# Two outlook-attention layers: first copies and zeros ahead of the loop, two weights' tables, a first normalisation on two engines, held projections

## The chip, the cores and the metric

The kernel runs on one core of one Trainium2 chip. The core has five engines that run their own instruction streams: TensorE (PE, with its weight loads shown apart as PEld), VectorE (DVE), ScalarE (ACT), GpSimd (POOL) and SyncE (SP), which here does nothing but issue DMAs. They wait for one another through semaphores. The metric is the device time of one execution in microseconds; lower is better. Here it was 3481.11 us, the median of 3 runs (3480.89 to 3484.68).

## The reference: what is computed

The input x is 8 images of 56 x 56 tokens with 384 channels, in float32. Two layers follow one another, each with a residual, and each works on a group normalisation of its input (32 groups of 12 channels, mean and variance over a whole image):

```python
x = x + L0(gn(x))
x = x + L1(gn(x))

# L0: 12 heads of 32 channels, 3x3 neighbourhoods on both sides (9 x 9 weights per head)
v = x @ Wv.T ; v_unf = the 3x3 neighbourhood of v (zero padded)        # (b, n, 9, 12, 32)
attn = softmax((x @ Wa.T).reshape(b, n, 12, 9, 9) * 32 ** -0.5)         # over the last axis
out = einsum('bnhpq,bnqhd->bnphd', attn, v_unf)                         # 9 results per token
y = fold(out)       # each of the 9 is added at its neighbour's place
return y @ Wo.T

# L1: 6 heads of 64 channels, one result per token
a = softmax((x @ W_attn + b_attn).reshape(b, n, 6, 9))
y = einsum('bpKhd,bphK->bphd', 3x3 neighbourhoods of (x @ W_v + b_v), a)
return y @ W_proj + b_proj
```

In both layers a result pixel is therefore a weighted sum of v over a small neighbourhood (5 x 5 in layer 0, after the fold; 3 x 3 in layer 1), with weights of its own for each pixel and head.

## The kernel before

**Units of work.** Images are taken in pairs (4 pairs). A pair has R = 112 rows (two images of 56) and W = 56 columns. A step of layer 0's loop (line 901) is one column of one pair, so the loop has 4 x 56 = 224 steps and 3 more for what lags behind (`LAG`). A column has 112 tokens and a matmul takes 128, so 7 columns carry the eighth along and every eighth step has no attention matmuls of its own (`NTILE`). What a column's weights and values are used for is a *patch*: PX = 7 columns of a pair, 8 patches to a pair, 32 in all. Layer 1 walks over the same 32 patches as groups of 7 steps.

**Tables in DRAM.** A weighted sum over a neighbourhood is computed as matmuls whose stationary side is a weights' matrix that is mostly zero. It is made by writing weights into a table in DRAM with one arrangement and reading it back with another. `vtab0` and `vtab1` hold values with zero margins, `ztab0[n]` and `ztab1[n]` weights; patch number n of a layer uses weights' table n modulo `NTAB` (3), lines 738, 781, 1113 and 1130. Before a table is used, its margins and gaps must be zero: `clear_v` (line 218, 3 DMAs) and `clear_weights` (line 229, 6 DMAs) send them from a tile of zeros on SP's queue. `clears` (line 239) lists at which step of layer 0's loop which table is cleared, and `upkeep` (line 855) issues what is due, one step at a time. Other tensors in DRAM: `xTs`, x transposed (channels on partitions); `x1s`, the result of layer 0; `lgtab`, layer 1's logits; `lasts`, parts of the eighth columns.

**The start.** Pair 0 is loaded in 14 blocks of 4 columns (672 KB each), transposed on TensorE and kept in SBUF, each block in a place that something else uses later: the tiles `wts`, z, vp, yT, xres, x1t (`homes`, line 489). `keep_block` (line 467) sends a block to `xTs` in DRAM; in the loop `upkeep` sends two in each of steps 0 to 6. At steps 1 and 8 GpSimd zeroes `wts` and the two z tiles, which the blocks must have left. After the last block, `norm_params` (line 269) turns the statistics into a scale and a bias for each channel and image (its square root is ScalarE's, line 298), and `normed` (line 568) applies them: blocks 0 and 1 ahead of the loop (lines 898 and 899), on ScalarE, in pieces of a chunk of 128 channels and one image.

**A step of layer 0.** `attend` (line 591) does three thirds of the attention logits of a column (`bank<-wa_t,xn`, three matmuls over the chunks of channels for each third, six in the profile's count) and its values (`bank<-wv_t,xn`). In the gaps between them `between(n)` (line 921) puts other work: the transposes of the next pair's x (`pt<-ident,xr`; the block xr is loaded by `stats_load` on SP's queue, every third step, one block ahead), the softmax's normalisation and the sums of neighbouring columns on GpSimd (`normalise`, `presum`), the sum over rows by matmul (`pw<-pre,shift`, in `fold`, three steps behind), the write of the weights (`ztab<-wts`) and jobs.

**Jobs.** `Jobs` (line 357) is a queue of closures with a due step; only its head is looked at, and a call `jobs.run(step, n)` runs at most n of those that are due. A step of layer 0 has two or three such places. `fetch` (line 771) reads a patch's weights (`z<-ztab`) and adds its jobs: 4 contractions (`pc<-z,vp`), 6 projections (`po<-yT,wo_t`, each followed on VectorE by the residual's sum `x1t<-po,xres`) and, for a pair's last patch, the next layer's parameters. `later` holds DMAs that are issued at the end of a step.

**The boundary and layer 1.** The last patch of layer 0 is fetched inside layer 1's loop: `last` (line 954) is called at step 0 of it with a due step 5 later (line 1209), so that its jobs and layer 1's first ones share one queue. A step of layer 1 (line 1200) has two places for jobs and one column of projections (`bank<-wc_t,xn`, values and logits together). The logits of a group go to DRAM when the group is done (`keep_logits`, at m = 0 of the next), are read back by rows (`read_logits`), weighed and shared out on VectorE and ScalarE, summed over rows on TensorE (`pw` in `move`, at m = 5), written to `ztab1`, and read as z two groups later.

**What sets the order.** Nearly every instruction is issued through `InOrder` or a helper with `keep_in_program_order`, so each engine and each queue does its work in the order of the program's text; a scheduler places only the few that are not. SP's queue carries nearly all DMAs, in order, and a waiting one holds up what is behind it. GpSimd's queue carries the values' spreads (`vtab<-v`), ScalarE's the logits and layer 1's weights. Line 134 in the profile is that helper, and line 215 is `fill`.

Of the kernel before, what the change touches and what calls it, by code (L numbers as in the profile page):

```python
# [8 lines left out]
F32 = mybir.dt.float32  # L9
AF = mybir.ActivationFunctionType  # L10
# [5 lines left out]
def two_outlook_layers(  # L16
# [35 lines left out]
    P = 128  # L52
# [41 lines left out]
    EP1, FIRST1 = 11, 4  # L94
    SLOT0, SLOT1 = EP0 * ROW0, EP1 * ROW1
    LINE0, LINE1 = SX0 * SLOT0 + ROW0, SX1 * SLOT1 + ROW1
    NTAB = 3

    xf = x.rearrange("b y x c -> (b y) x c")
    of = out.rearrange("b y x c -> (b y) x c")  # L100
# [108 lines left out]
    def fill(table, first, dims, width):  # L209

        src = zeros[: dims[0][1], :width]
        if len(dims) > 1:
            src = src.unsqueeze(1).to_broadcast([dims[0][1], dims[1][1], width])
        tc.keep_in_program_order(
            nc.sync.dma_start(bass.AP(table.tensor, table.offset + first, [*dims, [1, width]]), src)
        )

    def clear_v(table, sx, pad):

        line = sx * C  # L220
        part = line // 12
        fill(table, 0, [[(R + GAP) * line, NPX + 1], [part, 12 * GAP]], part)
        fill(table, GAP * line, [[line, R], [C, pad]], C)
        fill(
            table, ((NPX - 1) * (R + GAP) + GAP) * line + (sx - pad) * C,
            [[line, R], [C, pad]], C,
        )

    def clear_weights(table, line, part, sx, slot, row, first, e, ep):
# [6 lines left out]
        fill(table, top + first * row, [[slot, sx]], row)  # L236
        fill(table, top + (R - 1) * line + (first + e - 1) * row, [[slot, sx]], row)

    def clears():

        yield 3, lambda: clear_v(vtab0, SX0, 2)

        yield 4, lambda: fill(
            ztab0[0], MARGIN * LINE0 + FIRST0 * ROW0, [[LINE0, R], [SLOT0, 2]], E0 * ROW0
        )
        for n, t in enumerate(ztab0):
            yield (5, 2 * PX, 3 * PX)[n], lambda t=t: clear_weights(
                t, LINE0, 366, SX0, SLOT0, ROW0, FIRST0, E0, EP0
            )
        yield 4 * PX, lambda: clear_v(vtab1, SX1, 1)  # L250
        for n, t in enumerate(ztab1):
            yield (5 + n) * PX, lambda t=t: clear_weights(
                t, LINE1, 350, SX1, SLOT1, ROW1, FIRST1, K, EP1
            )

# [8 lines left out]
    def weight(pool, src, n, name, queue=nc.sync):  # L264
        t = pool.tile([P, NCH, n], F32, name=name)
        queue.dma_start(t, src.rearrange("(i p) n -> p i n", p=P))
        return t
# [153 lines left out]
    def layer0(late, pools):  # L421
# [93 lines left out]
        for blk in range(NBLK):  # L515
            if blk + NXR - 1 < NBLK:
                first_load(blk + NXR - 1)
            for i in range(NCH):
                for _ in stats_chunk(0, blk, i):
                    pass  # L520
            if blk == 1:
                wv_t = weight(fixed, wv0, C, "wv0_t", sync)
        for _ in norm_params(stats.pop(0), "0_0", params, 0):
            pass

# [39 lines left out]
                xTs[pair][:, :, blk * XB * R : (blk + 1) * XB * R],  # L565
            )

        def normed(g, chunks, whole=True, shared=True):

            scale, bias = params[g // NBLK]  # L570
            xin, to = xins[g], xns[g // 2 % 2]
            for i in chunks:
                for b in range(IMG):
                    rows = slice(b * H, (b + 1) * H)

                    def put(dst, src):
                        scalar.activation(
                            dst, src, AF.Identity,
                            bias=bias[:, i, b : b + 1], scale=scale[:, i, b : b + 1],
                        )  # L580

                    n = XB - g % 2
                    if whole:
                        put(to[:, i, g % 2 * XB : g % 2 * XB + n, rows], xin[:, i, :n, rows])
                    if shared and g % 2:
                        put(
                            to[:, i, :, R + b * PART : R + (b + 1) * PART],
                            xin[:, i, n, rows].rearrange("p (j y) -> p j y", j=NTILE),
                        )
# [178 lines left out]
                lambda: sync.dma_start(xres[pair, px], xTs[pair][:, :, px * T : (px + 1) * T])  # L768
            )

        def fetch(pair, px, due):

            nm = f"0_{pair}_{px}"
            n_tile = 2
# [64 lines left out]

            for half in range(2):  # L840
                for j in range(NCH):
                    jobs.add(due, lambda half=half, j=j: project_out(half, j))
            if px == NPX - 1:
                def params_part(n):
                    if n == 0:
# [9 lines left out]
        def upkeep(step):  # L855

            pair, c = divmod(step, W)
            if pair == 0:

                for n in (2 * step, 2 * step + 1):  # L860
                    if n < NBLK:
                        keep_block(0, (0, 1, 4, 2, 3)[n] if n < 5 else n)
                if c == 1:
                    gpsimd.memset(wts, 0.0)
                if c == 3:
                    sync.dma_start(wo_t, wo0.rearrange("(i p) n -> p i n", p=P))
                if c == 8:
                    for z in zs:
                        nc.gpsimd.memset(z, 0.0)
            while clearing and clearing[0][0] <= step:  # L870
                clearing.pop(0)[1]()
            if pair + 1 < NPAIR:
                blk, i = divmod(c - 3, NCH)
                if 0 <= c and i == 0 and blk < NBLK - 1:
                    stats_load(pair + 1, blk + 1, sync, xr_tile(pair + 1, blk + 1))
                if NBLK * NCH + 3 <= c < NBLK * NCH + 6:
                    if c == NBLK * NCH + 3:
                        making["0"] = norm_params(stats.pop(pair + 1), f"0_{pair + 1}", params, pair + 1)
                    next(making["0"])
            g, j = divmod(step + 2 * XB, XB)  # L880
            if j < NCH and g < NPAIR * NBLK:
                normed(g, (j,))
            if step < NCH:
                normed(1, (step,), shared=False)
            if j == NCH - 1 and 2 < g + 1 < NPAIR * NBLK and g > 2:
                load(g + 1)
# [8 lines left out]

        vector.on = scalar.on = True
        xins.update({blk: homes[blk] for blk in range(4)})
        normed(0, range(NCH))
        normed(1, range(NCH), whole=False)
        LAG = 3  # L900
        for step in range(NPAIR * W + LAG):
            folding = fold(*divmod(step - LAG, W)) if step >= LAG else iter(())
# [3 lines left out]
            def weigh():  # L906
# [11 lines left out]
                if normal:  # L918
                    keep_v(*divmod(step - 1, W))

            def between(n):

                if n == 0:
                    next(turning, None)
                    weigh()
                    jobs.run(step, 1)
                elif n == 1:
                    next(folding, None)
                    next(turning, None)
                elif n == 2:  # L930
                    jobs.run(step, 1)
                else:
                    for part in summing:
                        next(part)
                    next(folding, None)
                    if step % SB == NTILE:
                        jobs.run(step, 1)
# [15 lines left out]

        def last(due):
            fetch_v(NPAIR - 1, NPX - 1)
            fetch(NPAIR - 1, NPX - 1, due)

        return step + 1, last, late_w

# [329 lines left out]
```

## Time and profile before

| What | Value |
|---|---|
| median of 3 runs | 3481.11 us (3480.89 to 3484.68) |
| the profiled execution | 3478.32 us, span 3476.5 us, mean clock 0.963 |
| TensorE busy | 3228.9 us, 93% |
| TensorE waiting for xr (`pt`), whole run | 46.7 us in 8 waits |
| TensorE waiting for GpSimd's pre (`pw`), whole run | 49.0 us in 16 waits |
| first matmul of layer 0's loop | at 65.99 us |
| layer 0's last patch and layer 1's first group | about 2225 to 2360 us |
| DMA | 859.13 MB, mean 247 GB/s |
| DMA share, 60 to 80 us | 0.00 |

How to read it: a line of the timeline has the start in us, the length in us, the engine (SPq is SP's queue issuing), the line of the program, the operation, what it writes and reads, and in brackets the idle time just before it with the work that ended that wait. A line of the waits has total, number and longest. A row of the windows has the stretch, its length, the busy time and count of each engine, the granted clock of TensorE, the DMA engines' busy share and GB/s. The totals of engines are means over stages that differ: TensorE is busy for nine tenths or more of most slices of the span, and for less at the start, around the boundary of the layers and at the end.

### The profile page before, as it was taken

How to read it: one execution, taken by the hardware profiler on the slowest of the kernel's cores; microseconds unless marked ns; L12 is line 12 of the kernel's file. 1: busy time of each engine (PE TensorE's matmuls, PEld its weight loads, DVE VectorE, ACT ScalarE, POOL GpSimd, SP SyncE). 2: the span in 40 equal slices, each digit the busy share in tenths (PEclk: the TensorE clock that was granted, in tenths of full speed). 3: DMA queues.
4: the chain of work that ended last, by engine and by line, in shares of the span. 5: the costliest groups of instructions: out<-in, count | busy, mean ns of one | idle time of the engine just before them, and what ended most of it. 6: DMA issues, size and time to landing. Idle time of an engine off the chain costs nothing. (4 is left out here: it accounts for less than half of the span.)

```text
span 3476.5 us, 74347 instructions
## 1 busy us (share of the span) xinstructions
PE 3228.9 (93%) x28510; PEld 2202.7 (63%) x28510; DVE 1873.0 (54%) x4780; ACT 1369.4 (39%) x3755; POOL 1367.7 (39%) x1982
## 2 busy tenths in 40 slices
PE   7688999999999998999998999888999999999998
PEld 5456666666666666666666666645666665656665
DVE  5556766666777666677666767532333332323331
ACT  4333444344444343444433443323434333433432
POOL 2544545544545454445454555421222222222220
PEclk7899999999999999999999999998999999999998
DMA  6788988887888687879766868768787878787875
GB/s 184 233 284 287 310 284 260 276 281 253 289 285 298 221 273 266 302 257 301 262 198 215 300 227 267 260 236 216 208 236 207 235 208 226 218 218 220 233 210 140
DMA packets 595753, 859.13 MB, mean 247 GB/s; under 512 B 205798, under 2 KB 470950, under 8 KB 591302
## 3 DMA queue, kind: packets, MB, share of 16 engines
q1 hardware_dynamic: 476806, 682.87, 62.6%
q0 software_dynamic: 59136, 148.12, 13.5%
q10 hardware_dynamic: 59456, 23.40, 2.9%
q8 instruction: 224, 3.67, 0.5%
q14 instruction: 131, 1.07, 0.1%
HBM read 520.28 MB, written 330.40 MB: 245 GB/s over the span
## 5 line engine op out<-in xcount | busy, mean ns | idle before, releaser
L119 PE MATMUL bank<-wa_t,xn 128*128 128x288 f32 x3528 | 981.3, 417 | 7.4 <-ACT xn L134 6.1
L119 PE MATMUL po<-yT,wo_t 128*128 128x448 f32 (+1 forms) x2304 | 827.1, 499 | 27.1 <-DVE x1t L134 24.5
L134 POOL TENSOR_TENSOR at<-at,den 128x972 f32<-128x972 f32 x196 | 440.6, 2248 | 932.8 <-DVE den L134 527.8
L119 PEld LDWEIGHTS bank<-wa_t,xn 128*128 128x128 f32 x3528 | 656.8, 194 | 222.8 <-issue 25.3
L119 PEld LDWEIGHTS po<-yT,wo_t 128*128 128x128 f32 x2304 | 428.9, 192 | 316.9 <-issue 187.8
L134 ACT ACTIVATE at<-at 128x972 f32<-128x972 f32 (+1 forms) x228 | 215.4, 945 | 963.1 <-DVE at L134 962.7
L332 POOL DMA_DIRECT2D vtab<-v x392 | 213.3, 548 | 845.5 <-DVE v L134 801.8
L119 PE MATMUL bank<-wc_t,xn 128*128 128x438 f32 x1176 | 481.9, 546 | 0.0
L134 DVE TENSOR_REDUCE mx<-bank 128x36 f32<-128x324 f32 x588 | 285.0, 485 | 346.2 <-PE bank L119 342.5
L119 PE MATMUL pc<-z,vp 121*32 121x49 f32 (+1 forms) x17664 | 386.0, 221 | 65.5 <-ACT yT L134 25.3
L119 PEld LDWEIGHTS pc<-z,vp 121*32 121x32 f32 (+1 forms) x17664 | 346.7, 123 | 137.6 <-issue 88.9
L119 PE MATMUL bank<-wv_t,xn 128*128 128x384 f32 x1176 | 423.4, 497 | 0.0
L134 DVE TENSOR_TENSOR at<-bank,mx 128x324 f32<-128x324 f32 x588 | 291.3, 495 | 170.9 <-ACT pre L134 58.8
L119 PEld LDWEIGHTS bank<-wc_t,xn 128*128 128x128 f32 x1176 | 216.3, 193 | 171.6 <-issue 165.0
L119 PEld LDWEIGHTS bank<-wv_t,xn 128*128 128x128 f32 x1176 | 222.8, 193 | 137.4 <-issue 15.8
L134 POOL DMA_DIRECT2D vtab<-v x476 | 289.8, 612 | 22.1 <-DMA vtab<-zeros 11.4
L134 ACT COPY yT<-pc 128x294 f32<-128x294 f32 (+2 forms) x512 | 196.5, 406 | 238.5 <-PE pc L119 237.6
L134 POOL TENSOR_TENSOR pre<-at,at 112x108 f32<-112x108 f32 (+1 forms) x440 | 224.3, 527 | 92.6 <-DMA at<-last 59.3
L134 DVE SCALAR_TENSOR_TENSOR x1t<-po,bo_t,x1t 128x448 f32<-128x448 f32 (+1 forms) x156 | 97.6, 626 | 249.4 <-PE po L119 249.4
L134 DVE TENSOR_TENSOR lgt<-bank,ba_t 128x54 f32<-128x54 f32 x196 | 41.7, 213 | 350.2 <-PE bank L119 350.2
L134 ACT ACTIVATE wts<-pre,inside 112x48 f32<-112x48 f32 (+4 forms) x672 | 181.0, 358 | 80.9 <-DMA ztab<-wts 48.3
L134 ACT COPY ot<-pt 112x384 f32<-112x384 f32 x128 | 61.4, 480 | 383.7 <-PE pt L122 334.2
(113 smaller groups left out, 3107.4 us busy)
## 6 DMA issues: line engine op xcount, KB each, us to landing
z<-ztab SPq DMA_DIRECT2D x64, 2352.0 KB
vp<-vtab SPq DMA_DIRECT2D x64, 1536.0 KB
vp<-vtab SPq DMA_DIRECT2D x64, 945.0 KB
xres<-xT SPq DMA_DIRECT2D x32, 1176.0 KB
ztab<-wts SPq DMA_DIRECT2D x336, 110.2 KB
vtab<-v POOLq DMA_DIRECT2D x108, 336.0 KB, 6.4
xin<-xT SPq DMA_DIRECT2D x52, 672.0 KB
xr<-in_x SPq DMA_DIRECT2D x50, 672.0 KB
```

The source lines that it names most:

```text
L119: tc.keep_in_program_order(nc.tensor.matmul(*args, **kwargs))
L134: return lambda *args, **kwargs: tc.keep_in_program_order(op(*args, **kwargs))
L332: queue.dma_start(bass.AP(table.tensor, table.offset + first, [*([line * step, count] for step, count in rows_of or ((1, rows),)), *([[(R ...
```

## The change

- `NTAB` becomes 2: two weights' tables a layer instead of three, so two clears fewer.
- Pair 0's 14 blocks are sent to `xTs` ahead of layer 0's loop, in a row, where the loop sent two in each of steps 0 to 6. Behind them, still ahead of the loop, `clear_first` sends the zeros of `vtab0` and of `ztab0[0]` (formerly at steps 3, 4 and 5).
- `ztab0[1]` is cleared at step 3 (formerly 14). The clears of `vtab1` and of the two `ztab1` come in pair 3, at steps 172, 178 and 186 (formerly 28, 35, 42 and, for the third table, 49).
- A square root of one column of constants is added on ScalarE ahead of the last statistics.
- The first normalisation goes chunk by chunk over both blocks, image 0 on ScalarE and image 1 on VectorE (`both=True`).
- At steps 221 and 222 no jobs run (`held_back`), and the projections of layer 0's last patch are due 9 steps (`PX + 2`) later than its other jobs (`final`).
- The scheduler's order also differs in one place that the text doesn't show: the zeroing of the first z tile on GpSimd comes at step 1, amid that step's spreads, where it came at step 5; the second stays.

```diff
--- before.py
+++ after.py
@@ -94,7 +94,7 @@
     EP1, FIRST1 = 11, 4
     SLOT0, SLOT1 = EP0 * ROW0, EP1 * ROW1
     LINE0, LINE1 = SX0 * SLOT0 + ROW0, SX1 * SLOT1 + ROW1
-    NTAB = 3
+    NTAB = 2
 
     xf = x.rearrange("b y x c -> (b y) x c")
     of = out.rearrange("b y x c -> (b y) x c")
@@ -236,20 +236,20 @@
         fill(table, top + first * row, [[slot, sx]], row)
         fill(table, top + (R - 1) * line + (first + e - 1) * row, [[slot, sx]], row)
 
+    def clear_first():
+
+        clear_v(vtab0, SX0, 2)
+        fill(ztab0[0], MARGIN * LINE0 + FIRST0 * ROW0, [[LINE0, R], [SLOT0, 2]], E0 * ROW0)
+        clear_weights(ztab0[0], LINE0, 366, SX0, SLOT0, ROW0, FIRST0, E0, EP0)
+
     def clears():
 
-        yield 3, lambda: clear_v(vtab0, SX0, 2)
-
-        yield 4, lambda: fill(
-            ztab0[0], MARGIN * LINE0 + FIRST0 * ROW0, [[LINE0, R], [SLOT0, 2]], E0 * ROW0
+        yield 3, lambda: clear_weights(
+            ztab0[1], LINE0, 366, SX0, SLOT0, ROW0, FIRST0, E0, EP0
         )
-        for n, t in enumerate(ztab0):
-            yield (5, 2 * PX, 3 * PX)[n], lambda t=t: clear_weights(
-                t, LINE0, 366, SX0, SLOT0, ROW0, FIRST0, E0, EP0
-            )
-        yield 4 * PX, lambda: clear_v(vtab1, SX1, 1)
+        yield (NPAIR - 1) * W + 4, lambda: clear_v(vtab1, SX1, 1)
         for n, t in enumerate(ztab1):
-            yield (5 + n) * PX, lambda t=t: clear_weights(
+            yield (NPAIR - 1) * W + 10 + 8 * n, lambda t=t: clear_weights(
                 t, LINE1, 350, SX1, SLOT1, ROW1, FIRST1, K, EP1
             )
 
@@ -520,6 +520,11 @@
                     pass
             if blk == 1:
                 wv_t = weight(fixed, wv0, C, "wv0_t", sync)
+        for blk in (1, 4, 0, 2, 3, *range(5, NBLK)):
+            keep_block(0, blk)
+        clear_first()
+        warm = stat.tile([P, 1], F32, tag="warm", name="warm", bufs=1)
+        scalar.activation(warm, eps_t, AF.Sqrt)
         for _ in norm_params(stats.pop(0), "0_0", params, 0):
             pass
 
@@ -565,7 +570,7 @@
                 xTs[pair][:, :, blk * XB * R : (blk + 1) * XB * R],
             )
 
-        def normed(g, chunks, whole=True, shared=True):
+        def normed(g, chunks, whole=True, shared=True, both=False):
 
             scale, bias = params[g // NBLK]
             xin, to = xins[g], xns[g // 2 % 2]
@@ -574,6 +579,12 @@
                     rows = slice(b * H, (b + 1) * H)
 
                     def put(dst, src):
+                        if both and b:
+                            vector.tensor_scalar(
+                                dst, src, scale[:, i, b : b + 1], bias[:, i, b : b + 1],
+                                ALU.mult, ALU.add,
+                            )
+                            return
                         scalar.activation(
                             dst, src, AF.Identity,
                             bias=bias[:, i, b : b + 1], scale=scale[:, i, b : b + 1],
@@ -768,7 +779,7 @@
                 lambda: sync.dma_start(xres[pair, px], xTs[pair][:, :, px * T : (px + 1) * T])
             )
 
-        def fetch(pair, px, due):
+        def fetch(pair, px, due, final=None):
 
             nm = f"0_{pair}_{px}"
             n_tile = 2
@@ -839,7 +850,7 @@
 
             for half in range(2):
                 for j in range(NCH):
-                    jobs.add(due, lambda half=half, j=j: project_out(half, j))
+                    jobs.add(due if final is None else final, lambda half=half, j=j: project_out(half, j))
             if px == NPX - 1:
                 def params_part(n):
                     if n == 0:
@@ -856,10 +867,6 @@
 
             pair, c = divmod(step, W)
             if pair == 0:
-
-                for n in (2 * step, 2 * step + 1):
-                    if n < NBLK:
-                        keep_block(0, (0, 1, 4, 2, 3)[n] if n < 5 else n)
                 if c == 1:
                     gpsimd.memset(wts, 0.0)
                 if c == 3:
@@ -895,8 +902,9 @@
 
         vector.on = scalar.on = True
         xins.update({blk: homes[blk] for blk in range(4)})
-        normed(0, range(NCH))
-        normed(1, range(NCH), whole=False)
+        for i in range(NCH):
+            normed(0, (i,), both=True)
+            normed(1, (i,), whole=False, both=True)
         LAG = 3
         for step in range(NPAIR * W + LAG):
             folding = fold(*divmod(step - LAG, W)) if step >= LAG else iter(())
@@ -918,17 +926,19 @@
                 if normal:
                     keep_v(*divmod(step - 1, W))
 
+            held_back = NPAIR * W - 4 < step < NPAIR * W - 1
+
             def between(n):
 
                 if n == 0:
                     next(turning, None)
                     weigh()
-                    jobs.run(step, 1)
+                    jobs.run(step, 0 if held_back else 1)
                 elif n == 1:
                     next(folding, None)
                     next(turning, None)
                 elif n == 2:
-                    jobs.run(step, 1)
+                    jobs.run(step, 0 if held_back else 1)
                 else:
                     for part in summing:
                         next(part)
@@ -953,7 +963,7 @@
 
         def last(due):
             fetch_v(NPAIR - 1, NPX - 1)
-            fetch(NPAIR - 1, NPX - 1, due)
+            fetch(NPAIR - 1, NPX - 1, due, due + PX + 2)
 
         return step + 1, last, late_w
```

## The prediction

> **What bounds the kernel now.** I read the engine totals first, then the waits of TensorE by releaser, then the timelines of TensorE and of the queue that it waited for, and last the windows of the first 500 us.
>
> ```profile
> PE 3228.9 (93%) x28510; PEld 2202.7 (63%) x28510; DVE 1873.0 (54%) x4780; ACT 1369.4 (39%) x3755; POOL 1367.7 (39%) x1982
> PEclk7899999999999999999999999998999999999998
> ```
>
> TensorE is the bound: 247.6 us of the span are not its own, and the clock drops at the start, at the boundary of the layers and at the end. No instruction of TensorE is removed, so the change can only be worth stalls and the slow clock behind them. The waits of TensorE from 60 to 460 us (pair 0 and the start of pair 1; total, times, longest):
>
> ```profile
> PE pt L122 <- DMA xr<-in_x: 44.2, 6, 11.3
> PE pw L119 <- POOL pre L134: 14.5, 4, 9.1
> ```
>
> These two are 58.7 us, about half of the run's large waits. Where they stand on TensorE:
>
> ```profile
> 98.14 0.55 PE L122 MATMUL pt<-ident,xr 112*128 112x112 f32 x4
> 98.53 1.63 PE L119 MATMUL bank<-wa_t,xn 128*128 128x288 f32 x6
> 122.65 0.98 PE L122 MATMUL pt<-ident,xr 112*128 112x112 f32 x4 [9.85 <-DMA xr<-in_x]
> 123.42 3.11 PE L119 MATMUL bank<-wa_t,xn 128*128 128x288 f32 x6
> 147.66 1.14 PE L119 MATMUL pw<-pre,shift 112*112 112x120 f32 x4 [9.07 <-POOL pre L134]
> 217.41 0.98 PE L122 MATMUL pt<-ident,xr 112*128 112x112 f32 x4 [11.19 <-DMA xr<-in_x]
> 318.37 1.01 PE L122 MATMUL pt<-ident,xr 112*128 112x112 f32 x4 [11.34 <-DMA xr<-in_x]
> 534.22 4.85 PE L119 MATMUL po<-yT,wo_t 128*128 128x448 f32 x6 [4.88 <-DVE x1t L134]
> ```
>
> Behind a stall of 10 us the same work runs slower: the four transposes 0.98 us for 0.55, the six matmuls 3.11 for 1.63. So a long stall costs about 2 us more than its own length. (The Trainium skill, "TensorE: Matmul & The Clock Gate", Part 1, says that an idle window of about 3.4 us halves the clock until about 3.4 us have been busy. That would be 1.7 us for each stall, and my sum about 2 us less.)
>
> What SP's queue issued ahead of the late loads:
>
> ```profile
> 106.09 4.35 SPq L215 DMA_DIRECT2D vtab<-zeros  x3
> 110.55 3.85 SPq L134 DMA_DIRECT2D xr<-in_x  x1
> 205.79 1.30 SPq L134 DMA_DIRECT2D xr<-in_x  x1
> 298.29 6.98 SPq L215 DMA_DIRECT2D ztab<-zeros  x6
> 305.37 1.96 SPq L134 DMA_DIRECT2D xr<-in_x  x1
> ```
>
> The loads of 122.65 and 318.37 stand right behind a clear. The one of 217.41 (issued at 205.79) doesn't: ahead of it are the patch's vp (180.94) and z (198.26), which the change leaves. The pw at 147.66 waited for GpSimd, with two memsets of the z tiles before it; the second can only start when the copies that read those tiles have landed. The start is on ScalarE:
>
> ```profile
> 60.18 1.28 ACT L298 ACT_TABLE_LOAD   x1 [9.45 <-DVE gvar L282]
> 62.30 2.89 ACT L134 ACTIVATE xn<-wts,bias,scale 128x224 f32<-128x224 f32 x6 [0.52 <-DVE bias L302]
> ```
>
> And the DMA engines stand idle just then (busy shares and the granted clock; the last two numbers are DMA share and GB/s):
>
> ```profile
> 60.00:80.00 20.00, 14.01 (x43) 10.24 (x44) 6.20 (x16) 10.86 (x21) 0.00 (x0) 0.70 0.00 1
> 100.00:150.00 50.00, 29.03 (x112) 20.85 (x111) 21.45 (x55) 14.59 (x40) 31.91 (x35) 0.80 0.79 236
> ```
>
> **The change part by part** (us gained; bounds in brackets).
>
> *First normalisation and Sqrt's table.* The table load, 1.28, leaves the path between gvar (59.94) and std; the other table load at 67.16 stays. The 6+6 activations (2.89 + 2.04) are split between two engines and ordered by chunk, so TensorE can start when chunk 0 is done: std at 60.2 for 61.5, bias 0.56 behind its end, then a sixth of 4.93, 0.8: near 62, not 65.99. Gain 4. The added activation stands ahead of ScalarE's copies and waits for a memset of GpSimd that ends at 8.9; the first copy was at 8.96, and that stretch is bound by loads (DMA share 0.98 up to 50 us): nothing. VectorE's six added pieces run while it is waiting for matmuls.
>
> *Keeps and first clears ahead of the loop.* The 14 copies (672 KB) took 1.65 us apiece when they followed the loads: keeps landed at 49.20 and 50.83. The last now lands near 49.2+13×1.65 = 70.7, in time that was idle, and no longer holds up z's memset. SP issues them in 14×0.6 and the clears in 14 (4.35, 1.49, 8.16), between 49 and 83, when it used to stand before last<-at (issued 83.29 once GpSimd was done); that small copy is now behind them, and nothing needs it before step 8. Behind them come the clears of vtab0 and ztab0[0], and only then xr(1,0), on the same queue. At 106 the first fill (9x36 rows) took 9.6 us to land, the two after it about 4, the large fill of ztab0 8.1 with 2.8 before it. Fills that overlap the keeps end earlier, so I put the end of the clears at 92–95 and xr(1,0) at 96, where TensorE, 4 earlier than now, wants it at 86 (89.97−3.8). So a new wait of about 10 at step 3, with 2 of slow clock; bounds 5 (the fills overlap the keeps) and 14. (The Trainium skill, "DMA: Bandwidth & Descriptors", Queues, rings and completion order, says that each DMA engine consumes a queue's descriptors in ring order. This speaks against the change: by it the load can't pass keeps or zeros, as my sum has it; a load that passed them would be worth 12 more.) Against that, the wait of 9.85 at 122.65 goes with its 2: xr(1,1) has only ztab0[1]'s small fills ahead and should land by 119.5, for a need near 121. GpSimd's 11.39 wait for the zeros (its spread at 117.92) goes too. Start to step 6 in all: 4−12+12−1 = **+3** (−5 to +10).
>
> *Memsets of z.* One of two (4.01) moves to step 1, where GpSimd's order is behind by 3 but TensorE is waiting for xr. The waits of pw, 2.05 and 9.07 with 1 of slow clock, become the 3.7 that the other memset (4.03) leaves: **+8.4** (5 to 9). The wait for xr at 159.85, 5.21 plus 1.8 of slow clock, followed from the same jam: **+7** (4 to 7.5).
>
> *Clears of steps 14, 21, 28.* 217.41 keeps its 11.19, slightly worse as TensorE arrives earlier: **−1** (−3 to +8). At 245.26, 2.62 and 1.7 of slow clock (at<-last stood behind the clear of 225): **+4.3** (2 to 5). At 318.37 the third table's clear is gone altogether: 11.34 + 1.7: **+13** (8 to 14). At 377.28 1.11: **+1**. At 534.22 the vector engine waited 5.43 for a DMA behind a clear: 4.88 and 4.85−2.52 of slow clock: **+7** (3 to 7.5).
>
> *Clears moved to pair 3.* Three clears (vtab1, two ztab1) now stand among pair 3's work at steps 172 to 186. Where they stood, the four of layer 1 cost between 0 (578) and 7.2 (534). In pair 3 there is no xr behind them, but z, vp, at<-last and xin are: **−3** (−8 to 0).
>
> *Two tables, not three.* A write of weights to a table now follows its reads by two patches. In layer 0 SP has already waited, for its own lanes, on reads that were issued earlier; in layer 1 the next weights' write after a z read (2586.40) comes at 2616.03 and goes to the other table. **0** (−3 to 0).
>
> *Held projections and the boundary.* Four projections move from the steps where pw_52 and pw_53 stalled 6.72 and 2.66 (2243–2249), to behind them; layer 1's first jobs come three slots (1.5 steps) later. The 12.37 wait for vp at 2355.60 should go, as contraction comes 1.5 steps later, but pw of group 0 then waits for the way through the table: lgtab written at 2302.65, read back from 2313.07, landed 2318.6, weighed 2321.3, with less matmul work to cover it. The two are within 1 of one another. **+3** (−6 to +8).
>
> *Layer 1.* The slots stay full, so the shift lasts. From the logits' write to pw was 22.9 us in the steady state (2591.14 to 2614.06), and I count 24.7 us of TensorE work between them before and 25.4 after: **0** (−8 to +5). In the tail the waits of 2.03 and 5.34 (3412–3420) have three projections more to hide them: **+4.5** (0 to 7).
>
> Sum: 3+8.4+7−1+4.3+13+1+7−3+0+3+0+4.5 = **47**. The profiled execution took 3478.3 (span 3476.5), so 3431 on its scale; the median of the runs stands 2.8 above it: **3434**.
>
> **The rivals.**
>
> *A. Given back in pair 0* (0.22). The stalls move: DMA share was already 0.79 to 0.93 in 100–350, so an earlier TensorE meets the same loads later. For it: two of six xr waits (217 and 436) have no clear ahead. Against: 60–80 us had no transfers at all. Then the gains at 159, 245, 318 and 534 (31.3) shrink to a third and the new wait at step 3 is 14: 47−21−4 = 22, so 3459; bounds 3452 to 3472.
>
> *B. Slower: layer 1 waits in every group* (0.10). The chain logits, table, softmax, pw has only 1.8–2.5 us of slack. If the new places of the projections push the reads of the logits (behind a load that waits for a buffer) so that pw stands 3 us per group, 31 groups cost 93, less 47 gained: slower by 46, 3527. It decides from 47/31 = 1.5 us per group. Against: the count above, and waits for pw that are nearly absent in steady layer 1.
>
> *C. Nothing to tell* (0.05). The clears do in pair 3 what those of pair 0 did (7.2 at 534, 13 at 318: 20 instead of 3) on top of A: 22−17 = 5, so 3476.
>
> **How the numbers follow.** A measurement of this kernel tells about 0.2% (7 us) from no change. Forecast 0.63: 3434, own range 3414 to 3454 (the terms' bounds added as independent, root of the squares, come to 14 up and 18 down; taken as 20). A 0.22, B 0.10, C 0.05. Range 3408 to 3470: it leaves out B, C, A's upper end and a little of the forecast below, 0.2 in all. Faster 0.84, same 0.06 (C and A's end), slower 0.10.
>
> **What would show it.** TensorE's first matmul near 62; waits for pt fewer than 30 us between 60 and 460, among them a new one near 90 and the old one at the tenth step of patch 2 (217); none near 318 less the gain; the wait for vp at the boundary gone, one for pw in its place. In the clock rows 100:150 should rise from 0.80. It is wrong if pw waits in each group of layer 1, if the first xr lands after 100, or if pair 3 shows waits behind the zeros.

## The result and the profile after

The changed kernel takes 3502.72 us (median of 4 runs, 3500.61 to 3509.42) where the kernel before took 3482.89 in the same comparison: ratio 1.0067, 95% interval 1.0038 to 1.0096. It is 20 us slower; the forecast was 47 us faster. The profiled execution has a span of 3498.6 us.

Engine totals and granted clock of the changed kernel:

```profile
PE 3245.2 (93%) x28510; PEld 2193.7 (63%) x28510; DVE 1866.6 (53%) x4786; ACT 1354.1 (39%) x3749; POOL 1367.7 (39%) x1982
PEclk8899999999999999999999999899999999999998
```

The same 28510 matmuls now keep TensorE busy for 16.3 us more (3228.9 before), though the clock at the start is better. So somewhere else it ran slower. TensorE's waits for x's blocks and for GpSimd, 60 to 460 us (total, times, longest), are 35.2 us, where they were 58.7:

```profile
PE pt L122 <- DMA xr<-in_x: 26.0, 4, 11.2
PE pw L119 <- POOL pre L134: 9.2, 2, 6.3
```

The start on TensorE's timeline:

```profile
60.05 6.83 PE L119 MATMUL bank<-wa_t,xn 128*128 128x288 f32 x18 [2.05 <-ACT xn L134]
94.59 0.98 PE L122 MATMUL pt<-ident,xr 112*128 112x112 f32 x4 [11.21 <-DMA xr<-in_x]
120.52 0.57 PE L122 MATMUL pt<-ident,xr 112*128 112x112 f32 x4 [2.37 <-DMA xr<-in_x]
141.46 1.14 PE L119 MATMUL pw<-pre,shift 112*112 112x120 f32 x4 [6.25 <-POOL pre L134]
205.17 0.98 PE L122 MATMUL pt<-ident,xr 112*128 112x112 f32 x4 [10.82 <-DMA xr<-in_x]
```

The loop's first matmul comes at 60.05 for 65.99. The new wait at step 3 is there (94.59), and the one of patch 2 stays (205.17); the wait of 11.34 before 318 is gone. Two stretches by engine (columns as in the prediction):

```profile
60.00:80.00 20.00, 19.95 (x68) 14.22 (x69) 11.91 (x28) 9.12 (x17) 5.74 (x3) 0.89 0.81 257
100.00:150.00 50.00, 38.40 (x157) 27.77 (x156) 28.16 (x72) 20.19 (x54) 28.88 (x36) 0.90 0.65 201
```

The DMA engines now work from 60 to 80 us (share 0.81 for 0.00), and the clock from 100 to 150 is 0.90 for 0.80. The start did what was forecast. Where the time went is seen when the same piece of work is compared by its start in both traces. "Lead" is by how much the changed kernel is ahead; in layer 0 by GpSimd's normalisation of a column, in layer 1 by pw of a group. Here and below, leads, waits and windows are from one profiled execution of each kernel:

| Place | Lead, us |
|---|---|
| step 8 | 5.3 |
| step 16 | 14.3 |
| step 24 | 27.8 |
| step 48 | 40.9 |
| step 112 | 34.1 |
| step 184 | 33.3 |
| step 192 | 25.6 |
| end of layer 0's loop | 31.2 |
| layer 1, pw of group 0 | 43.9 |
| group 2 | 32.7 |
| group 16 | 7.0 |
| group 30 | −18.5 |
| end | −22.1 |

Layer 1 loses 51 us in 28 groups, 1.8 us in each. From pw of group 2 to pw of group 30 (2402.9 to 3389.7 before, 2370.2 to 3408.2 after) the waits of TensorE are, in the kernel before:

```profile
PE pc L119 <- ACT yT L134: 11.7, 13, 2.0
```

and in the changed one:

```profile
PE pw L119 <- DVE at L134: 29.7, 20, 1.9
PE bank L122 <- ACT ot L134: 9.8, 10, 1.7
PE po L119 <- ACT yT L134: 3.0, 3, 1.0
```

The windows of the same stretch, before:

```profile
2402.90:3389.70 986.80, 975.06 (x7502) 610.27 (x7500) 307.30 (x653) 390.04 (x1144) 218.06 (x402) 0.99 0.80 221
```

and after:

```profile
2370.20:3408.20 1038.00, 996.08 (x7500) 610.50 (x7500) 299.00 (x653) 379.44 (x1144) 217.12 (x400) 0.97 0.75 209
```

Of the 51.2 us, 30.2 are idle time (41.9 for 11.7) and 21.0 are the same matmuls running longer at a lower clock. One group of the changed kernel on TensorE shows both:

```profile
2701.43 0.54 PE L122 MATMUL bank<-ident,z 128*112 128x128 f32 x3 [1.29 <-ACT ot L134]
2703.82 1.60 PE L119 MATMUL pw<-at,shift 112*112 112x126 f32 x6 [1.85 <-DVE at L134]
2705.21 4.59 PE L119 MATMUL bank<-wc_t,xn 128*128 128x438 f32 x6
2711.36 2.37 PE L119 MATMUL bank<-wc_t,xn 128*128 128x438 f32 x6
```

Two waits of 1.29 and 1.85 us, and the six matmuls behind them take 4.59 us, where they take 2.37 six microseconds later. A wait of 1.85 us that stands alone has no such effect here:

```profile
2779.42 0.91 PE L119 MATMUL pw<-at,shift 112*112 112x126 f32 x6 [1.85 <-DVE at L134]
2780.17 2.37 PE L119 MATMUL bank<-wc_t,xn 128*128 128x438 f32 x6
```

What they wait for, on SP's queue and on VectorE:

```profile
2679.21 1.33 SPq L134 DMA_DIRECT2D x1t<-x  x1
2694.51 0.31 SPq L134 DMA_DIRECT2D at<-lgtab  x1
```

```profile
2699.03 0.84 DVE L134 TENSOR_REDUCE mx<-at 112x42 f32<-112x378 f32 x1 [6.41 <-DMA at<-lgtab]
2700.96 1.03 DVE L134 SCALAR_TENSOR_TENSOR z<-po,bo_t,z 128x336 f32<-128x336 f32 x2
2703.21 0.55 DVE L134 TENSOR_TENSOR at<-at,den 112x378 f32<-112x378 f32 x1
```

The group's logits went to DRAM at 2678.77. The read waits for that write, as in all 28 groups (SP's own waits in this stretch):

```profile
SPq L134 <- DMA lgtab<-lgt: 320.4, 28, 14.9
```

In this one the next group's x1t (1.2 MB) is ahead of the read on the queue, VectorE begins the softmax 20.3 us after the write, and two residual sums stand between its pieces. ScalarE's exponent stands ahead of its copies of the output (`ot`), so these are late with it.

### The profile page after: what moved, and what is told of

It reads as the page before. It is cut to its first block, busy times and chain, and to the rows that moved or that the text cites. A ratio compares the mean times of both kernels' runs of the same rounds, so it can differ in the third digit from the quotient of the medians.

```text
span 3498.6 us, 74335 instructions
## 1 busy us (share of the span) xinstructions
PE 3245.2 (93%) x28510; PEld 2193.7 (63%) x28510; DVE 1866.6 (53%) x4786; ACT 1354.1 (39%) x3749; POOL 1367.7 (39%) x1982
## 5 line engine op out<-in xcount | busy, mean ns | idle before, releaser
L134 ACT ACTIVATE xn<-xin,bias,scale 128x168 f32<-128x168 f32 (+1 forms) x474 | 208.5, 504 | 0.0
```

What stands on the lines that cost most here:

```text
L134: return lambda *args, **kwargs: tc.keep_in_program_order(op(*args, **kwargs))
```

## The experiments

Theory 1: the later due time of the last patch's projections moves all jobs of layer 1 by three slots for good, and this makes layer 1 wait. Theory 2: two tables instead of three slow the weights' write or read in layer 1. The kernel before was measured again in each comparison; the ratios are against it.

**own_due**: the due time as before, jobs still held at steps 221 and 222.

```diff
-            fetch(NPAIR - 1, NPX - 1, due, due + PX + 2)
+            fetch(NPAIR - 1, NPX - 1, due)
```

> The changed kernel with one part undone: the last patch's projections are due with its other jobs again (layer 1's jobs go back by three slots); no jobs at steps 221 and 222 still. Theory 1 (the three slots make layer 1 wait): groups of layer 1 go back from 36.8 us to about 35.0 each, the waits of pw for the softmax (35.1 us in the changed kernel) fall under 10, and the time is 3440 to 3460. Theory 2 (two weights' tables instead of three make layer 1 slow): no change in the groups, 36.5 us or more each, time within 10 us of 3503. Theory 3 (both parts): in between, groups near 35.9, 3470 to 3485.

3451.32 us (3440.31 to 3454.53), ratio 0.9913 (0.989 to 0.9936). The windows from pw of group 2 to pw of group 30:

```profile
2375.90:3363.70 987.80, 973.61 (x7505) 609.70 (x7501) 307.23 (x653) 389.46 (x1144) 217.89 (x402) 1.00 0.79 221
```

35.3 us a group again (987.8 / 28), clock 1.00, and of TensorE's waits only one kind is left:

```profile
PE pc L119 <- ACT yT L134: 14.2, 16, 2.2
```

This one line is what turned a gain of 29 us into a loss of 20.

**no_hold**: jobs at steps 221 and 222, the late due time kept.

```diff
-            held_back = NPAIR * W - 4 < step < NPAIR * W - 1
+            held_back = False
```

> The changed kernel with jobs allowed at steps 221 and 222 again, the late due time kept. Theory 1 with the late due time alone as its cause: layer 1 stays at 36.5 us or more a group, and the time is 3500 to 3512, as only the four projections at the end of layer 0 go back before pw (its waits there, 6.7 and 2.7 in the kernel before, come back). If the held jobs are what shifts layer 1's slots: groups near 35, time under 3470.

3501.88 us (3494.99 to 3508.9), ratio 1.0064 (1.0039 to 1.0089); 37.2 us a group. The held jobs are not what shifts layer 1. In the changed kernel they win 4.5 us of lead from step 216 to the loop's end (26.7 to 31.2), here 0.1; at the end of the kernel nothing of it can be told.

**three_tables**: three tables, the third of layer 0 cleared at step 14 and that of layer 1 at step 194 (the clears' list puts it there; the expectation below says 202).

```diff
-    NTAB = 2
+    NTAB = 3
+        yield 2 * PX, lambda: clear_weights(
+            ztab0[2], LINE0, 366, SX0, SLOT0, ROW0, FIRST0, E0, EP0
+        )
```

> The changed kernel with three weights' tables a layer (the third of layer 0 is cleared at step 14, the third of layer 1 at step 202), all else as changed. Theory 2: layer 1's groups go back to 35.0 us, time near 3450 plus what two more clears cost (0 to 15). Theory 1: groups stay at 36.5 us or more, time 3503 to 3518.

3506.94 us (3505.05 to 3509.99), ratio 1.0081 (1.006 to 1.0102); 37.1 us a group. Theory 2 falls.

**before_late_due**: the kernel before with the late due time alone (`fetch` takes `final` as in the change).

```diff
-            fetch(NPAIR - 1, NPX - 1, due)
+            fetch(NPAIR - 1, NPX - 1, due, due + PX + 2)
```

> The kernel before with one part of the change alone: the last patch's projections due nine steps later. Theory 1: layer 1's groups go from 35.0 to about 36.8 us and the waits of pw for the softmax appear (30 us or more); time 3483 plus 57 less some 12 won at the boundary (the wait for vp of 12.4): 3520 to 3535. Theory 2: groups stay at 35, time 3465 to 3483.

3534.9 us (3528.21 to 3540.14), ratio 1.0158 (1.0136 to 1.018); 37.4 us a group. Its waits from group 2 to group 30:

```profile
PE pw L119 <- DVE at L134: 31.9, 22, 1.9
PE bank L122 <- ACT ot L134: 13.2, 11, 3.9
PE po L119 <- ACT yT L134: 3.0, 3, 1.0
```

The due time alone brings the whole loss, on either kernel. Next: why three slots cost 1.8 us a group. Theory 1a: the way of the logits (write, read, softmax) has no slack, and the load ahead of the read is part of it. Theory 1b: it is something else in the new order of the jobs.

**late_load_behind**: the changed kernel, late due time kept, with the read ahead of the load in layer 1's step.

```diff
-            if m == 1 and g + 1 < NG:
-                load(g + 1)
             if g > 1 and m == 0:
                 ...
             if g and m == read:
                 read_logits(done)
+            if m == 1 and g + 1 < NG:
+                load(g + 1)
```

> The changed kernel with one pair of DMAs exchanged on SP's queue in layer 1: a group's logits are read back first, and the next group's x1t (1.2 MB) is loaded behind them, not ahead. Slots and jobs stay as changed. Theory 1a (pw waits because the way of the logits through the table, 19.6 us from write to VectorE's mx, has no slack, and the load is part of that way): the way shortens by 2 to 4 us, the waits of pw for the softmax fall from 29 us to under 8, groups go from 37.1 to 35.0 to 35.6 us, time 3440 to 3465. Theory 1b (the three slots cost through something else, such as TensorE's order itself or copies on ScalarE): groups stay over 36.5 us, time over 3490.

3432.49 us (3424.89 to 3440.39), ratio 0.9867 (0.9843 to 0.9891). SP's queue, waits and windows from pw of group 2 to group 30:

```profile
2663.60 0.31 SPq L134 DMA_DIRECT2D at<-lgtab  x1
2664.07 0.42 SPq L134 DMA_DIRECT2D x1t<-x  x1
```

```profile
PE pw L119 <- DVE at L134: 3.9, 7, 0.9
PE po L119 <- ACT yT L134: 3.0, 3, 1.0
```

```profile
2357.30:3332.30 975.00, 967.71 (x7502) 597.87 (x7501) 299.65 (x652) 384.90 (x1145) 217.38 (x400) 1.00 0.81 223
```

With the slots unchanged, 70 us came back by an exchange of two DMAs: 34.8 us a group, and a time 8 us below the range forecast for 1a. 1a holds.

**own_load_behind**: the same exchange on own_due.

> The changed kernel with the last projections' own due time and the same exchange of DMAs. Theory 1a: here TensorE's waits for ScalarE's yT (19.5 us in 17 waits) are the same late logits in another place, since ScalarE's exponent stands ahead of those copies; they go too, groups fall from 35.3 to 34.3 to 34.8 us, time 3425 to 3442. Theory 1b: no change from 3451, within 6 us.

3432.07 us (3426.06 to 3438.57), ratio 0.9866 (0.9843 to 0.9888). From pw of group 2 to that of group 30 TensorE has no idle time at all, so 34.6 us is what a group's matmuls take:

```profile
2369.30:3338.40 969.10, 969.10 (x7504) 607.43 (x7500) 308.29 (x652) 394.62 (x1144) 217.36 (x401) 1.00 0.81 224
```

The waits for yT that own_due has there were the late logits too, as expected. With the exchange the late due time costs nothing and wins nothing.

**before_load_behind**: the exchange on the kernel before.

> The kernel before with the exchange alone (logits read back ahead of the next load in layer 1). If the kernel before already paid for the late logits, under the name of ScalarE's copies (waits for yT of 18.3 us in layer 1): those go to about 5, groups from 35.25 to 34.6 us, 15 to 22 us faster: 3458 to 3466. If its way of the logits was fully covered: within 5 us of 3480.

3452.34 us (3448.39 to 3472.7, 10 runs), ratio 0.9922 (0.9897 to 0.9948), 34.6 us a group and no waits of TensorE between groups 2 and 30. The kernel before already paid some 18 us for the logits (35.25 − 34.61 a group, over 28). The median lies 6 us below the forecast for this case, within the scatter of these runs.

**late_pw_m6**: the changed kernel with softmax and pw one step later in each group.

```diff
-            read, first, second, moved = (0, 2, 3, 4) if last else (1, 3, 4, 5)
+            read, first, second, moved = (0, 2, 3, 4) if last else (1, 4, 5, 6)
```

> The changed kernel with weigh, share and pw of layer 1 each one step later in a group (m = 4, 5, 6 for 3, 4, 5); slots as changed. Theory 1a: some 5 us more of matmuls cover the way of the logits, the waits of pw for the softmax are gone, groups 35.0 to 35.6 us; z is then read sooner after its write, so waits of pc for z or vp may come: time 3445 to 3475. Theory 1b: groups stay over 36.5 us.

3449.3 us (3438.16 to 3453.85), ratio 0.9912 (0.9882 to 0.9942), 35.6 us a group. No wait of pw is left, but 17 us for yT are:

```profile
PE pc L119 <- ACT yT L134: 11.0, 15, 1.8
PE po L119 <- ACT yT L134: 6.1, 3, 2.0
```

It agrees with 1a from the other side: not a shorter way, but more work beside it.

The means over the groups (from the timelines: issue of the logits' write, VectorE's first instruction on what is read back, pw) put numbers on the way:

| Kernel | write to VectorE's mx | mx to pw | write to pw | a group |
|---|---|---|---|---|
| before | 19.3 | 4.8 | 24.1 | 35.25 |
| own_due | 19.4 | 4.8 | 24.2 | 35.28 |
| after | 19.6 | 4.9 | 24.6 | 37.07 |
| own_load_behind | 16.3 | 7.3 | 23.7 | 34.61 |
| late_load_behind | 17.9 | 5.5 | 23.4 | 34.82 |
| late_pw_m6 | 22.5 | 4.9 | 27.5 | 35.56 |

These are estimates from means over groups that differ (from write to pw 22.1 to 27.9 us before, 21.7 to 27.7 after). Where TensorE doesn't wait (own_load_behind), 23.7 us of its work lie between write and pw; in the late slots 23.3 (23.4 less 0.1 of waits). Softmax needs at least 4.3 us from mx to pw in the kernel before and 4.8 in most groups after, where two residual sums stand between. Before: 19.3 + 4.3 = 23.6 needed, 23.7 there. After: 19.6 + 4.8 = 24.4 needed, 23.3 there. What is short shows as 1.5 us of waits a group (42.5 / 28), and 0.75 us of slow clock behind them (21.0 / 28). The count gives the sign and most of the size; the 0.4 us between 1.1 and 1.5 it doesn't account for.

**own_xr_first**: on own_due, the first block of pair 1 is loaded ahead of the first clears (and no longer at step 0).

```diff
             keep_block(0, blk)
+        stats_load(1, 0, sync, xr_tile(1, 0))
         clear_first()
```

> The changed kernel with the last projections' own due time, and xr(1,0) loaded ahead of the first clears instead of behind them. If the 11.2 us wait at 94.6 us is the clears ahead of the load on the queue: it goes, the first pw comes 8 to 13 us earlier than at 98.3, and the time is 3438 to 3447. If the start is bound by the transfers as a whole (the clears then hold the spreads of vtab0 or the first weights' writes): another wait of 5 to 10 us takes its place within the next six steps, time 3447 to 3455.

3440.38 us (3436.08 to 3448.96), ratio 0.9892 (0.987 to 0.9915). The wait for xr is gone; one of 4.36 for GpSimd comes instead, and pw is 9 us earlier:

```profile
89.27 1.14 PE L119 MATMUL pw<-pre,shift 112*112 112x120 f32 x4 [4.36 <-POOL pre L134]
113.07 0.57 PE L122 MATMUL pt<-ident,xr 112*128 112x112 f32 x4 [1.64 <-DMA xr<-in_x]
```

At step 16 its lead over own_due is 9 us, at step 48 1.5, at step 192 3. Most of it meets later waits, and the 11 us between the medians are more than its trace accounts for.

**own_old_start**: own_due without the second engine and the early square root in the first normalisation.

```diff
-        warm = stat.tile([P, 1], F32, tag="warm", name="warm", bufs=1)
-        scalar.activation(warm, eps_t, AF.Sqrt)
...
-        for i in range(NCH):
-            normed(0, (i,), both=True)
-            normed(1, (i,), whole=False, both=True)
+        normed(0, range(NCH))
+        normed(1, range(NCH), whole=False)
```

> The changed kernel with the last projections' own due time, and the first normalisation and the square root's table as they were (both blocks on ScalarE in turn, no earlier square root). As the prediction's sum has it, the 4 us of the start are given back at the wait for xr(1,0) (11.2 us at 94.6 us), since the transfers set its end: first matmul of the loop 4 us later than at 60.05, that wait 7 to 8 us instead of 11.2, from step 8 on no difference over 2 us, time 3449 to 3455. If the 4 us last: 3455 to 3460 and a lead at step 16 that is smaller by 4.

3455.36 us (3448.84 to 3472.62, 10 runs), ratio 0.993 (0.9902 to 0.9957).

```profile
66.44 7.24 PE L119 MATMUL bank<-wa_t,xn 128*128 128x288 f32 x18 [6.08 <-ACT xn L134]
96.20 0.98 PE L122 MATMUL pt<-ident,xr 112*128 112x112 f32 x4 [6.01 <-DMA xr<-in_x]
```

The first matmul is 6.7 later than own_due's (59.73), the wait at step 3 is 4.5 shorter than its 10.53, and at step 16 the lead differs by 1.9: most of the gain at the start is given back where the transfers set the end. By step 48 the leads differ by 7.1 again (34.1 for 41.2). This profiled execution took 3471.98 us, 17 over the kernel's median, and nothing in the edit explains what it loses later on; the median is 4 us from own_due's.

**late_behind_xr**: late_load_behind and own_xr_first together.

> Two earlier experiments together on the changed kernel (late due time kept): logits read back ahead of the next load in layer 1, and xr(1,0) loaded ahead of the first clears. If the two gains are independent, as their places (80 to 125 us, and 2300 us to the end) suggest: 3432 less 5 to 10, so 3420 to 3428. If the start's gain is taken back in layer 0's later pairs (with own due times it was 8 us at step 8 and only 3 at step 192): 3428 to 3434.

3430.15 us (3419.71 to 3438.05), ratio 0.985 (0.9794 to 0.9905). Against late_load_behind 2 us, within the scatter. The lead at step 48 is 6.7 us larger than without, at step 192 it is 8.8 smaller. Whether the start's gain is kept stays open, as this execution is the slowest of its four runs and late_load_behind's is the fastest.

**clears_later**: late_behind_xr with the three clears of pair 3 at steps 174, 181 and 188.

```diff
-        yield (NPAIR - 1) * W + 4, lambda: clear_v(vtab1, SX1, 1)
+        yield (NPAIR - 1) * W + 6, lambda: clear_v(vtab1, SX1, 1)
...
-            yield (NPAIR - 1) * W + 10 + 8 * n, lambda t=t: clear_weights(
+            yield (NPAIR - 1) * W + 13 + 7 * n, lambda t=t: clear_weights(
```

> The kernel of late_behind_xr with the three clears for layer 1 two steps behind a patch's read of z instead of just ahead of it or near it (steps 174, 181, 188 instead of 172, 178, 186). If the 8 to 10 us lost between steps 184 and 192 are the zeros ahead of z on SP's queue: 6 to 10 us faster than late_behind_xr, 3412 to 3420, and the lead over the kernel before stays level from step 184 to 192. If the zeros cost as traffic wherever they stand in pair 3: within 4 us of late_behind_xr.

3430.67 us (3414.18 to 3434.7), ratio 0.9844 (0.9788 to 0.99). The lead still falls from 35.1 to 27.7 between steps 184 and 192. A place two steps later changes little, so two more runs asked whether the zeros cost it at all.

**clears_pair0**: late_load_behind with the three clears back at steps 28, 35 and 42.

```diff
-        yield (NPAIR - 1) * W + 4, lambda: clear_v(vtab1, SX1, 1)
+        yield 4 * PX, lambda: clear_v(vtab1, SX1, 1)
...
-            yield (NPAIR - 1) * W + 10 + 8 * n, lambda t=t: clear_weights(
+            yield (5 + n) * PX, lambda t=t: clear_weights(
```

**clears_split**: late_load_behind with the weights' clears sent one fill to a step, at 173 to 178 and 179 to 184 (`clear_weights` takes the numbers of the fills that it sends).

```diff
-            yield (NPAIR - 1) * W + 10 + 8 * n, lambda t=t: clear_weights(
+            for k in range(6):
+                yield (NPAIR - 1) * W + 5 + 6 * n + k, lambda t=t, k=k: clear_weights(
-                t, LINE1, 350, SX1, SLOT1, ROW1, FIRST1, K, EP1
+                    t, LINE1, 350, SX1, SLOT1, ROW1, FIRST1, K, EP1, (k,)
```

> The kernel of late_load_behind with the three clears for layer 1 back in pair 0 (steps 28, 35 and 42, where the kernel before had its first three), so none in pair 3. If the 8 to 10 us that the lead loses from step 184 to 192 are those zeros: the lead stays level there (within 2 us), while in pair 0 the waits behind zeros come back (1 to 12 us less lead at step 48): time 3425 to 3438. If something else in the change costs them in pair 3 (two tables, the earlier arrival of TensorE): the loss of 8 to 10 stays at steps 184 to 192, time 3436 to 3448.

> The kernel of late_load_behind with the weights' clears for layer 1 sent one fill to a step (steps 173 to 178 and 179 to 184) instead of six at once. If it is the row of six on SP's queue that holds z and the weights' writes up: the loss at steps 184 to 192 falls from 9 to under 4 us, time 3422 to 3430. If the zeros' transfers cost as such: the loss stays 7 to 10 us over steps 168 to 192, time within 5 us of 3432.

| Lead at step | 32 | 48 | 184 | 192 | time, us | ratio |
|---|---|---|---|---|---|---|
| late_load_behind | 29.2 | 40.3 | 42.4 | 33.0 | 3432.49 | 0.9867 (0.9843 to 0.9891) |
| clears_pair0 | 29.6 | 30.0 | 28.6 | 28.7 | 3435.58 | 0.9873 (0.9847 to 0.9898) |
| clears_split | 28.3 | 41.1 | 39.4 | 39.1 | 3426.92 | 0.9858 (0.9841 to 0.9876) |

Without zeros in pair 3 the lead stays level there, and pair 0 loses 10 us instead. With one fill to a step in pair 3 it stays level between steps 184 and 192 too. Over all three clears, from step 168 to 192, the lead changes by +1.8 us without zeros, by −1.6 with one fill to a step and by −8.5 with rows of six. So the zeros of pair 3 are the price, 10 us in rows and 3 one by one, and most of the 10 is paid at one place: the lead of late_load_behind is 42.0 at step 188 and 34.2 at step 189, just behind the second table's row of six, which takes SP's queue 9.68 us:

```profile
1870.79 9.68 SPq L215 DMA_DIRECT2D ztab<-zeros  x6
```

The first table's row of six, at step 178, costs 0.5 us there (the lead goes from 40.0 at step 176 to 42.4 at 184, without zeros from 25.7 to 28.6; up to 3 us in the other kernels), and the one at step 181 in clears_later nothing. clears_split not only parted the second row, it also moved it from step 186 to 179 to 184. Whether the row or its place costs the 8 us is therefore not shown; a row of six for the second table at an earlier step wasn't run. clears_split is the fastest of all by its median: 1.4% faster than the kernel before, where the change as it was is 0.7% slower. Against late_load_behind its interval overlaps.

## Why the prediction was wrong

- **The step that failed: "Layer 1 ... From the logits' write to pw was 22.9 us in the steady state (2591.14 to 2614.06), and I count 24.7 us of TensorE work between them before and 25.4 after: 0 (−8 to +5)".** It measured −51 from group 2 to 30. The 22.9 was one group, of 22.1 to 27.9; the mean was 24.1, and most of that was TensorE's own time. The cover is 23.7 in the old slots and 23.3 in the new ones, not 24.7 and 25.4. The slack I called 1.8 to 2.5 us was about 0.1 before and −1.1 after, by these means. So the three slots took some 0.4 us of cover where the count had them add 0.7, and put two residual sums into the softmax (4.8 us for 4.3), which the count left out. The trace of before had a hint of it: TensorE's waits for yT (11.7 us between groups 2 and 30) were the softmax's delay under another name, as ScalarE does exponent and copies in one order. before_load_behind shows that, since these waits are gone there. I had taken only the tail's into the sum.
- **Rival B** had the mechanism, the place (pw) and the deciding point (1.5 us a group; measured 1.8), with its price too high (3). It laid the late read to a load that waits for a buffer; the read waits for its own write (11.4 us a group, 320.4 / 28), and late_load_behind shows that the load ahead of it lengthens the way. It got 0.10 because of that count and because the trace of before had next to no waits for pw.
- **The tail**, +4.5 in the sum, was −3.6 (lead from −18.5 at group 30 to −22.1): the waits of 2.03 and 5.34 went, and one of 10.82 came at 3438.58, before a transpose: the residual sum that it needs stands behind the last group's softmax on VectorE, which waited 12.20 us for the logits.
- **The start** was right in mechanism: first matmul at 60.05 (forecast 62), wait at step 3 11.21 (10), lead at step 8 5.3 (3). That most of the normalisation's gain is given back at that wait is shown by own_old_start (6.7 us later at the start, 1.9 at step 16).
- **Memsets of z** were mis-sized: waits of 2.98 and 6.25 stayed, for the 3.7 forecast. Lead behind them 6.2, forecast 11.4.
- **The waits at 159, 217, 245, 318, 377 and 534**: each went or stayed as forecast; 217's stays (10.82 at 205.17). The wait at 436 (5.53), priced at nothing, shrank to 1.60 as well, and so the lead at step 48 is 40.9 with 42.7 forecast.
- **Clears in pair 3**: −8 (33.3 to 25.6) for −3, at the forecast's lower bound; clears_pair0 shows the zeros as the cause.
- **Steps 48 to 184** lose 7.6 us that no term has. Other executions with the same instructions there lose 5 (own_due), nothing (no_hold) or gain 2 (late_load_behind), so nothing is concluded from it; its cause stays open.
- **Two tables**: 0, as forecast (three_tables). **Held jobs**: 4.5 of lead; the boundary as a whole, from step 216 to group 2, +6 for +3.

Without the late due time the sum's other parts give own_due's 29 us; the forecast for those (47 less 4.5 for the tail and 3 for the boundary) was about 40.

## What to carry to other kernels

A way that goes out through DRAM and back beside the matmuls has a slack; take it as a mean over the groups, from write to use, before work is moved in a full pipeline, since a shift of a slot is paid in every group. A wait can stand under the name of another instruction that shares an engine's order with the late one. And on a shared queue what is wanted first goes first: one exchange of a read and a load won about 0.8% on the kernel before and 2% on the changed one, and the change by itself lost 0.7%.

## What the runs showed of the hardware

- Waits far shorter than those at the start lower the clock too. In the changed kernel none of the 33 waits of the steady stretch is over 1.9 us, and the same 28 groups took 996.08 us of busy time for 975.06, at a granted clock of 0.97 for 0.99. Nearly all of it stands behind pairs of waits: behind each of the 10 pairs (a wait for ScalarE's ot, then one of pw, starting 1.9 to 2.5 us apart) the next six matmuls of 128x438 took 3.22 to 4.59 us instead of 2.37, and behind the 10 waits of pw that stand alone (0.17 to 1.85 us) only once (3.41). (The Trainium skill, "TensorE: Matmul & The Clock Gate", Part 1, ties the lower clock to an idle window of about 3.4 us. Here two gaps of 1.29 and 1.85 us, within 3.7 us, were enough; no run here shows the window itself.)
- The write of a group's logits (162 KB in 25 of 28 groups, in rows of 216 bytes) was complete, by the issue of its read, only 11.6 us after its own issue before and 14.3 after (means), while z, vp and x1t were on the DMA engines.
- A row of six fills with zeros on the shared queue has no fixed price: 8 us of TensorE's time at step 186 (42.0 to 34.2 of lead), 0.5 to 3 at step 178. The fills of both tables one to a step, at 173 to 184, cost 3 us together with vtab1's clear.
